# The first block of a time-mix and FFN kernel: parameters as rows, roots on ScalarE, mixing in eight steps

## The chip, the cores and the metric

The kernel runs on one core of a Trainium2 chip. It drives five engines that run side by side and wait for each other through semaphores: TensorE (PE in the profile; PEld is its weight load), VectorE (DVE), ScalarE (ACT), GpSimd (POOL) and SyncE (SP), which here issues every transfer from memory. The metric is the device time of one execution in microseconds (us). Smaller is better.

## The reference

Input x has 4 sequences of 1024 tokens with 512 channels. Cut to what matters:

```
xn  = layernorm(x)                               # no gamma, no beta
xx  = shift(xn) - xn                             # the token before; the first token takes the second
k   = (xn + xx * time_mix_k) @ Wk.T              # 512 -> 704
r   = (xn + xx * time_mix_r) @ Wr.T
state_t = state_(t-1) * exp(-exp(time_decay)) + relu(k_t)    # along time
att = layernorm((state * r) @ Wv.T) * ln_gamma + ln_beta
ffn = gelu(fp16(xn) @ W0.T + bias0).fp16 @ W1.T + bias1      # 512 -> 2048 -> 512
out = x + att + fp16(ffn)
```

## The kernel before

Tokens go through in eight blocks of 512, two per sequence. For each block channels lie on the partitions, so the normalized x must be turned. In blocks 1 to 7 VectorE does this in 32x32 pieces during the FFN of the block before. Block 0 has nothing to hide behind, and has a path of its own: TensorE turns 128x128 pieces into four PSUM banks `pts`, and the mixing reads these banks.

The loads at the start, all on one queue (cut):

```python
    x_now = load_x(0)                       # four transfers of 128 x 512
    ...
    nc.vector.memset(w_sb, 0.0)
    nc.sync.dma_start(mk_sb, mix_k.rearrange("(c p) -> p c", p=P))   # channel on the partition
    nc.sync.dma_start(mr_sb, mix_r.rearrange("(c p) -> p c", p=P))
    for c in range(NC):                     # NC = 4
        nc.sync.dma_start(wk_sb[c], wkT[c * P : (c + 1) * P, :])
        nc.sync.dma_start(wr_sb[c], wrT[c * P : (c + 1) * P, :])
    nc.sync.dma_start(w_sb[:, :NF], decay[:H0].rearrange("(c p) -> p c", p=P))
    nc.sync.dma_start(w_sb[:HF, NF:], decay[H0:].rearrange("(c p) -> p c", p=HF))
    nc.sync.dma_start(b0_sb, bias0.rearrange("(c p) -> p c", p=P))
```

The first block's statistics, normalization and mixing (cut):

```python
    def rstd_of(var, name):                 # 1/sqrt as a power, on GpSimd
        nc.gpsimd.tensor_scalar_add(r, var, EPS)
        nc.gpsimd.tensor_tensor(r, r, nhalf[:, :n], ALU.pow)

    # first_inputs: statistics of four tiles s on VectorE, rstd_of once for each two tiles
        for s in range(NS):                 # NS = 4
            normalize(xs[:, s, :], ...)     # VectorE, (x - mean) * rstd
            for c in range(NC):
                nc.tensor.transpose(pts[c][:, s * P : (s + 1) * P], xs[:, s, c * P : (c + 1) * P], ident)
        for rest, m in ((onemk_sb, mk_sb), (onemr_sb, mr_sb)):
            nc.vector.tensor_scalar(rest, m, -1.0, 1.0, ALU.mult, ALU.add)     # 1 - m
        for c, pt in enumerate(pts):
            parts = (xk with mk_sb, onemk_sb), (xnT with mr_sb, onemr_sb)      # shortened
            for dst, part, m, rest in parts:
                nc.scalar.activation(part, pt, AF.Identity, scale=rest)
            for dst, part, m, rest in parts:                                   # first token
                nc.scalar.activation(dst[:, 0:1], pt[:, 1:2], AF.Identity, bias=part[:, 0:1], scale=m)
            for dst, part, m, rest in parts:
                nc.vector.scalar_tensor_tensor(dst[:, 1:], pt[:, : TB - 1], m, part[:, 1:], ALU.mult, ALU.add)
```

Then ScalarE copies the banks to fp16 (`x16`) and their last column to `last`, takes the two exponentials of the decay, and the products of the attention begin. For each h of 5 there are four products for k, four for r; relu on ScalarE, the scan and the product with r on VectorE:

```python
        for h in range(NF):
            for c in range(NC):
                product(pk, wk_sb, cols, xk[:, c, :], c)
            st = states(h, P, pk)           # relu on ScalarE, scan on VectorE
            for c in range(NC):
                product(pr, wr_sb, cols, xnT[:, c, 1:], c)
            nc.vector.tensor_mul(g[:, h, :], st, pr)
        # then the last half h, both parts in one bank: pkr
```

PSUM has eight banks, used as two pools of four: `ps_mm` for products, `ps_e` for the turned x and later the FFN's output. Behind the weights of the attention, W0 and W1 come in as raw tiles of 128x512 (three buffers, `w0raw` and `w1raw`), and ScalarE and VectorE split each in two parts while the first attention runs:

```python
    def split(hi, lo, raw):
        nc.scalar.copy(hi, raw)
        nc.vector.tensor_sub(lo, raw, hi.bitcast(F32))
```

Of the kernel before, what the change touches and what calls it, by code (L numbers as in the profile page):

```python
# [9 lines left out]
F32 = mybir.dt.float32  # L10
F32R = mybir.dt.float32r
AF = mybir.ActivationFunctionType
ALU = mybir.AluOpType

P = 128
EPS = 1e-5
# [3 lines left out]
def time_mix_and_gelu_ffn(  # L20
# [26 lines left out]
    nc = tc.nc  # L47
# [3 lines left out]
    TB = 512  # L51
    NS = TB // P
    NC = C // P
    NN = N // P
# [3 lines left out]
    NF = HID // P  # L58
    H0 = NF * P
    HF = P // 2  # L60
# [3 lines left out]
    def pool(name, bufs, **kw):  # L64
        return ctx.enter_context(tc.tile_pool(name=name, bufs=bufs, **kw))
# [4 lines left out]
    const = pool("const", 1)  # L70
    one = pool("one", 1)
    two = pool("two", 2)
    three = pool("three", 3)
    four = pool("four", 4)
    ps_mm = pool("ps_mm", 4, space=bass.MemoryType.PSUM)
# [12 lines left out]
    ident = const.tile([P, P], F32, name="ident")  # L88
# [1 line left out]
    nhalf = const.tile([P, NS], F32, name="nhalf")  # L90
    nc.vector.memset(nhalf, -0.5)

    mk_sb = const.tile([P, NC], F32, name="mk_sb")
    mr_sb = const.tile([P, NC], F32, name="mr_sb")
    w_sb = const.tile([P, NF + 1], F32, name="w_sb")
    nc.vector.memset(w_sb, 0.0)
    b0_sb = const.tile([P, NN], F32, name="b0_sb")

    nc.sync.dma_start(mk_sb, mix_k.rearrange("(c p) -> p c", p=P))
    nc.sync.dma_start(mr_sb, mix_r.rearrange("(c p) -> p c", p=P))  # L100
    wk_sb = [const.tile([P, HID], F32, name=f"wk_{c}") for c in range(NC)]
    wr_sb = [const.tile([P, HID], F32, name=f"wr_{c}") for c in range(NC)]
    for c in range(NC):
        nc.sync.dma_start(wk_sb[c], wkT[c * P : (c + 1) * P, :])
        nc.sync.dma_start(wr_sb[c], wrT[c * P : (c + 1) * P, :])
    nc.sync.dma_start(w_sb[:, :NF], decay[:H0].rearrange("(c p) -> p c", p=P))
    nc.sync.dma_start(w_sb[:HF, NF:], decay[H0:].rearrange("(c p) -> p c", p=HF))
    nc.sync.dma_start(b0_sb, bias0.rearrange("(c p) -> p c", p=P))

    onemk_sb = const.tile([P, NC], F32, name="onemk_sb")  # L110
    onemr_sb = const.tile([P, NC], F32, name="onemr_sb")

    wv_sb = const.tile([P, NF + 1, C], F32, name="wv_sb")
    gamma_sb = const.tile([P, C], F32, name="gamma_sb")
    beta_sb = const.tile([P, C], F32, name="beta_sb")
# [48 lines left out]
    xnT = const.tile([P, NC, TB + 1], F32, name="xnT")  # L164
# [3 lines left out]
    def rstd_of(var, name):  # L168

        n = var.shape[1]  # L170
        r = two.tile([P, n], F32, tag=f"rstd{n}", name=name)
        nc.gpsimd.tensor_scalar_add(r, var, EPS)  # L172
        nc.gpsimd.tensor_tensor(r, r, nhalf[:, :n], ALU.pow)
        return r

    def stats_of(mv, s, src, name):
        st6 = two.tile([P, 6], F32, tag="st6", name=name)
        nc.vector.bn_stats(st6, src)  # L178
        nc.vector.bn_aggr(mv[:, s, :], st6)  # L179

    def normalize(dst, src, mean, rstd):
        nc.vector.tensor_scalar(dst, src, mean, rstd, ALU.subtract, ALU.mult)
# [21 lines left out]
    def first_inputs(xs, behind):  # L204

        pts = [ps_e.tile([P, TB], F32, tag="pe", name=f"pt_0_{c}") for c in range(NC)]
        mv = two.tile([P, NS, 2], F32, tag="mv", name="mvx_0")
        rstds = []  # L210
        with tc.manual_schedule(engines={nc.gpsimd.engine}):
            for s0 in range(0, NS, 2):
                for s in (s0, s0 + 1):
                    stats_of(mv, s, xs[:, s, :], f"stx_0_{s}")
                rstds.append(rstd_of(mv[:, s0 : s0 + 2, 1], f"rx_0_{s0}"))
        xk = one.tile([P, NC, TB], F32, tag="xk", name="xk_0")
        with tc.manual_schedule(engines={nc.scalar.engine, nc.vector.engine}):
            for s in range(NS):
                normalize(
                    xs[:, s, :],  # L220
                    xs[:, s, :],
                    mv[:, s, 0:1],
                    rstds[s // 2][:, s % 2 : s % 2 + 1],
                )
                for c in range(NC):
                    nc.tensor.transpose(
                        pts[c][:, s * P : (s + 1) * P], xs[:, s, c * P : (c + 1) * P], ident
                    )
            for rest, m in ((onemk_sb, mk_sb), (onemr_sb, mr_sb)):
                nc.vector.tensor_scalar(rest, m, -1.0, 1.0, ALU.mult, ALU.add)  # L230
            for c, pt in enumerate(pts):
                ar = two.tile([P, TB], F32, tag="xx", name=f"ar_0_{c}")
                parts = (
                    (xk[:, c, :], xk[:, c, :], mk_sb[:, c : c + 1], onemk_sb[:, c : c + 1]),
                    (xnT[:, c, 1:], ar, mr_sb[:, c : c + 1], onemr_sb[:, c : c + 1]),
                )
                for dst, part, m, rest in parts:
                    nc.scalar.activation(part, pt, AF.Identity, scale=rest)
                for dst, part, m, rest in parts:

                    scaled = nc.scalar.activation(
                        dst[:, 0:1], pt[:, 1:2], AF.Identity, bias=part[:, 0:1], scale=m
                    )
                for dst, part, m, rest in parts:
                    mixed = nc.vector.scalar_tensor_tensor(  # L245
                        dst[:, 1:], pt[:, : TB - 1], m, part[:, 1:], ALU.mult, ALU.add
                    )

        behind.enter_context(tc.issue_after(scaled.ins))
        behind.enter_context(tc.issue_after(mixed.ins))  # L250
        x16s = []
        for c, pt in enumerate(pts):
            x16 = four.tile([P, TB], F16, tag="x16", name=f"x16_0_{c}")
            nc.scalar.copy(x16, pt)
            x16s.append(x16)
            nc.scalar.copy(last[:, c, :], pt[:, TB - 1 :])
        return x16s, xk

    def mixed_inputs(i):
# [23 lines left out]
    def ffn_input(i, x16s):  # L283
        xf = wide.tile([P, NC, TB], F32R, tag="xf", name=f"xf_{i}")
        for c in range(NC):
            nc.vector.tensor_copy(xf[:, c, :], x16s[c])
        return xf
# [164 lines left out]

    behind = ExitStack()
    x16s, xk = first_inputs(x_now, behind)

    nc.scalar.activation(w_sb, w_sb, AF.Exp)
    nc.scalar.activation(w_sb, w_sb, AF.Exp, scale=-1.0)
    xf = ffn_input(0, x16s)
    for i in range(len(blocks)):
        more = i + 1 < len(blocks)  # L460
# [25 lines left out]
        if more:  # L486
            x16s, xk = state["mixed"]
# [46 lines left out]
```

## Time and profile before

| | |
|---|---|
| time, median of three runs | 949.51 us (948.9 to 949.73) |
| span of the profiled execution | 947.2 us |
| mean granted clock of TensorE | 0.997 |
| TensorE busy, matmul | 931.0 us, 98% |
| VectorE busy | 485.7 us, 51% |
| ScalarE busy | 160.5 us, 17% |
| GpSimd busy | 53.7 us, 6% |
| moved by DMA | 106.47 MB, mean 112 GB/s |

How to read what the prediction shows. In the page, a row of digits is the span in 40 equal slices, each digit the busy share in tenths. The chain of waits is followed back from the last instruction; each of its lines is a start, a duration and what ran or was waited for. A line of the timeline is a start, a duration, the engine, the source line, the operation, output<-inputs, shapes and a count; in brackets stands the idle time before it and what ended that. A product in fp32 appears as two matmul rows. Names such as `xk` stand for the program's tiles, and `L238` for a line of the program.

### The profile page before, as it was taken

Reading aid. Unit: us, or ns where it says so; the run is one execution under the profiler, and the core shown is the slowest. Engines: PE = TensorE matmul, PEld = TensorE weight load, DVE = VectorE, ACT = ScalarE, POOL = GpSimd, SP = SyncE. Lnnn points to the kernel's source line nnn. Section 1 sums busy time; section 2 is a strip of 40 time slices with the busy share of each in tenths; the row PEclk is TensorE's granted clock in tenths of the full one; section 3 lists DMA queues with packets and bytes.
Section 4 is the critical chain, followed back from the end, with each engine's and each line's share of the span. In section 5 each row is a group of like instructions: output and inputs, shape, how many; then the busy total and the mean of one; then the engine's idle time right before and its main releaser. Section 6 shows DMA issues by size and latency. Waiting matters only on the chain.

```text
span 947.2 us, 8658 instructions
## 1 busy us (share of the span) xinstructions
PE 931.0 (98%) x3216; PEld 583.0 (62%) x3216; DVE 485.7 (51%) x836; ACT 160.5 (17%) x264; POOL 53.7 (6%) x128
## 2 busy tenths in 40 slices
PE   5999999999999999999999999999999999999998
PEld 2447764478644785448854488545884458744686
DVE  6558852385424844259443593436924269232513
ACT  5322321012100121002201022010210102111021
POOL 1011000010001000011000100001000020000100
PEclk9999999999999999999999999999999999999999
DMA  8734570045400354004540155301542024410243
GB/s 271 240 133 145 209 268 1 0 134 199 157 0 21 136 186 148 0 24 142 190 134 1 33 165 180 111 1 57 184 161 88 0 80 143 160 62 0 69 153 111
DMA packets 43368, 106.47 MB, mean 112 GB/s; under 512 B 8256, under 2 KB 8256, under 8 KB 43328
## 3 DMA queue, kind: packets, MB, share of 16 engines
q1 hardware_dynamic: 43328, 105.94, 33.4%
q8 instruction: 25, 0.41, 0.2%
q14 instruction: 15, 0.12, 0.0%
HBM read 89.14 MB, written 16.78 MB: 112 GB/s over the span
## 4 chain that ended last, share of the span: by engine, by line
PE 93%; DVE 4%; ACT 1%; issue 1%; DMA 0%; POOL 0%; DVEq 0%
PE pd L408 23%; PE pe L423 22%; PE po L348 15%; PE pr L313 15%; PE pk L313 14%; PE pkr L313 3%; PE po L358 2%; DVE xnT L199 1%; DVE w L120 1%; DVE stx L178 0%; DVE d L418 0%; DMA x<-in_L_attn_x 0%; DVE z L395 0%; DVE e L394 0%; DVE xk L278 0%
## 5 line engine op out<-in xcount | busy, mean ns | idle before, releaser
L423 PE MATMUL pe<-w,d 128*128 128x512 f32 x1024 | 251.2, 390 | 1.4 <-DVE w L120 0.8
L423 PEld LDWEIGHTS pe<-w,d 128*128 128x128 f32 x1024 | 192.2, 188 | 42.4 <-DVE d L418 1.5
L408 PE MATMUL pd<-xf,w0h 128*128 128x512 f32 x512 | 203.8, 398 | 0.0
L408 PE MATMUL pd<-xf,w0l 128*128 128x512 f32 x512 | 199.9, 390 | 0.0
L416 ACT ACTIVATE d<-pd,b_sb 128x512 f16<-128x512 f32 x128 | 87.9, 686 | 418.2 <-PE pd L408 399.2
L313 PE MATMUL pk<-xk,wk 128*128 128x512 f32 x320 | 145.9, 599 | 3.1 <-DVE xk L245 3.1
L313 PE MATMUL pr<-xnT,wr 128*128 128x512 f32 x320 | 144.0, 592 | 0.0
L348 PE MATMUL po<-wv_sb,g 128*128 128x512 f32 x320 | 140.8, 595 | 0.0
L418 DVE CAST d<-d 128x512 fp32r<-128x512 f16 x128 | 54.1, 424 | 130.7 <-ACT d L416 129.7
L408 PEld LDWEIGHTS pd<-xf,w0h 128*128 128x128 f32 x512 | 96.2, 188 | 28.0 <-issue 5.7
L408 PEld LDWEIGHTS pd<-xf,w0l 128*128 128x128 f32 x512 | 96.2, 188 | 21.6 <-issue 1.9
L313 PEld LDWEIGHTS pk<-xk,wk 128*128 128x128 f32 x320 | 61.0, 192 | 78.3 <-issue 70.9
L313 PEld LDWEIGHTS pr<-xnT,wr 128*128 128x128 f32 x320 | 60.7, 190 | 76.8 <-issue 76.1
L348 PEld LDWEIGHTS po<-wv_sb,g 128*128 128x128 f32 x320 | 60.2, 190 | 75.5 <-issue 74.8
L199 DVE STREAM_TRANSPOSE xnT<-x 32x512 f32<-32x512 f32 x112 | 78.7, 703 | 2.2
L300 DVE TENSOR_TENSOR_SCAN st<-w_sb,carry,rk 128x512 f32<-128x512 f32 (+1 forms) x24 | 30.8, 1282 | 70.2 <-ACT rk L298 70.2
L298 ACT ACTIVATE rk<-pk 128x512 f32<-128x512 f32 x40 | 24.0, 600 | 232.9 <-PE pk L313 232.9
L178 DVE BATCH_NORM_STATS2 sty<-po 128x6 f32<-128x512 f32 x32 | 22.1, 690 | 73.4 <-PE po L358 67.9
L300 DVE TENSOR_TENSOR_SCAN st<-w_sb,rk 128x512 f32<-128x512 f32 (+1 forms) x24 | 29.3, 1222 | 53.6 <-ACT rk L298 53.5
L324 DVE TENSOR_TENSOR g<-st,pr 128x512 f32<-128x512 f32 x40 | 27.5, 688 | 53.7 <-PE pr L313 53.6
L172 POOL TENSOR_SCALAR ry<-mvy 128x1 f32<-128x1 f32 x32 | 11.4, 357 | 503.4 <-DVE mvy L179 503.4
L313 PE MATMUL pkr<-xnT,wr 128*64 128x512 f32 x64 | 29.2, 598 | 0.0
(56 smaller groups left out, 439.6 us busy)
## 6 DMA issues: line engine op xcount, KB each, us to landing
w<-w1d SPq DMA_DIRECT2D x111, 512.0 KB, 3.2
x<-in_L_attn_x SPq DMA_DIRECT2D x32, 256.0 KB, 3.4
xres<-in_L_attn_x SPq DMA_DIRECT2D x32, 256.0 KB, 2.7
w1d<-w SPq DMA_DIRECT2D x16, 512.0 KB, 3.0
out<-z SPq DMA_DIRECT2D x32, 256.0 KB, 4.8
w0raw<-in_L_ffn_W SPq DMA_DIRECT2D x16, 256.0 KB, 4.5
w1raw<-in_L_ffn_W SPq DMA_DIRECT2D x16, 256.0 KB, 3.5
wk<-in_L_attn_Wk SPq DMA_DIRECT2D x4, 352.0 KB, 6.0
```

Of the source, the lines that this page charges most:

```text
L178: nc.vector.bn_stats(st6, src)
L199: nc.vector.transpose(dst[i * Q : (i + 1) * Q, :, :, j, :], src[j * Q : (j + 1) * Q, :, :, i, :],)
L298: nc.scalar.activation(rk[:hw], pk, AF.Relu)
L300: nc.vector.tensor_tensor_scan(st[:hw], w_sb[:hw, h : h + 1].to_broadcast([hw, TB]), rk[:hw], 0.0 if t0 == 0 else carry[:hw, h : h + 1], A ...
L313: nc.tensor.matmul(dst, w[c][:, cols], src, start=(c == 0), stop=(c == NC - 1))
L324: nc.vector.tensor_mul(g[:, h, :], st, pr)
L348: nc.tensor.matmul(pos[s], g[:, h, s * P : (s + 1) * P], wv_sb[:, h, :], start=(first and h == 0), stop=(not first and h == NF - 1),)
L358: nc.tensor.matmul(pos[s], gh[rows, s // 2, :], wv_sb[rows, NF, :], start=first, stop=not first)
L408: nc.tensor.matmul(pd, w[c][:, cols], xf[:, c, :], start=(c == 0 and w is w0h), stop=(c == NC - 1 and w is w0l),)
L416: nc.scalar.activation(d16, pd, AF.Gelu, bias=b0_sb[:, n : n + 1])
L418: nc.vector.tensor_copy(d, d16)
L423: nc.tensor.matmul(pe[s], d[:, s * P : (s + 1) * P], w1[part], start=(n == 0 and part == 0), stop=(n == NN - 1 and part == 1),)
```

## The change

It touches only the path of block 0, and what is loaded ahead of it. Its purpose is to bring the first product of the attention forward, and to keep TensorE's clock up until then.

- The mix vectors, the decay and bias0 are loaded as rows (4 to 16 rows of 128 values) right behind x, ahead of the weights, turned on TensorE and copied by ScalarE, where before they were loaded with the channel on the partition.
- The block's inverse deviations come from a square root on ScalarE and a reciprocal on VectorE. The table for the root is loaded by a first root that nothing reads. Tile 0 is normalized on ScalarE, the others on VectorE.
- The first token, which takes its neighbour from the other side, is treated by five small VectorE instructions on two columns that TensorE turned apart (`edge`), where before ScalarE had two one-column instructions for each c.
- The mixing goes in eight steps, one ScalarE and one VectorE instruction each, ordered so that the two engines read different banks: (c, kind) in the order of `steps`, kind 0 for k and 1 for r. The scheduler orders the first eight products to match: k of c = 0, 1, r of 0, 1, k of 2, 3, r of 2, 3.
- Nineteen products of the identity with itself go to a bank that nothing reads: 13 at the start, 1 behind tile 0, 5 behind tile 3.
- The four banks of `ps_mm` are taken by the unread products and the three turned parameters and edges first, then by the products of the attention. The exponentials of the decay move behind the copies of the banks.

The diff, cut:

```diff
+    eps_sb = const.tile([P, 1], F32, name="eps_sb")
+    mix_rows = const.tile([2 * NC, P], F32, name="mix_rows")
+    late_rows = const.tile([NF + 1 + NN, P], F32, name="late_rows")
-    nc.sync.dma_start(mk_sb, mix_k.rearrange("(c p) -> p c", p=P))
-    nc.sync.dma_start(mr_sb, mix_r.rearrange("(c p) -> p c", p=P))
+    nc.sync.dma_start(mix_rows[:NC], rows(mix_k))
+    nc.sync.dma_start(mix_rows[NC:], rows(mix_r))
+    nc.sync.dma_start(late_rows[:NF], rows(decay[:H0]))
+    nc.sync.dma_start(late_rows[NF : NF + 1, :HF], decay[H0:].rearrange("(c p) -> c p", p=HF))
+    nc.sync.dma_start(late_rows[NF + 1 :], rows(bias0))
     ...                                    # wk, wr as before
-    (decay and bias0 behind the weights)
 ...
+        def busy(n):
+            for _ in range(n):
+                nc.tensor.matmul(idle[:, :P], ident, ident, start=True, stop=True)
+        def deviations(s0):
+            nc.scalar.activation(rstd[:, s0 : s0 + 2], mv[:, s0 : s0 + 2, 1], AF.Sqrt, bias=eps_sb)
+        def inverses(s0):
+            nc.vector.reciprocal(rstd[:, s0 : s0 + 2], rstd[:, s0 : s0 + 2])
+        def normalized(s):                  # s == 0: shift0 on VectorE, then Identity on ScalarE
+        steps = [(0, 0), (1, 0), (0, 1), (1, 1), (2, 0), (3, 0), (2, 1), (3, 1)]
+            nc.scalar.activation(shift0, eps_sb, AF.Sqrt)
+            busy(13)
+            stats(0); stats(1); deviations(0); stats(2); inverses(0)      # one per line in the source
+            normalized(0); turned(0)
+            (edge: four transposes of two tokens)
+            busy(1)
+            stats(3); deviations(2); normalized(1)
+            nc.scalar.copy(ends, edge_t)
+            turned(1)
+            nc.tensor.transpose(mix_t, mix_rows, ident[: 2 * NC, : 2 * NC])
+            nc.scalar.copy(mix_sb, mix_t)
+            nc.scalar.activation(rest_sb, mix_t, AF.Identity, bias=1.0, scale=-1.0)
+            inverses(2); normalized(2); turned(2); normalized(3); turned(3)
+            nc.tensor.transpose(late_t, late_rows, ident[: NF + 1 + NN, : NF + 1 + NN])
+            busy(5)
+            (five small VectorE instructions for the first token)
+            for c, kind in steps:
+                nc.scalar.activation(part, pts[c][:, 1:], AF.Identity, scale=rest_sb[:, j : j + 1])
+                nc.vector.scalar_tensor_tensor(dst, pts[c][:, : TB - 1], mix_sb[:, j : j + 1], part, ALU.mult, ALU.add)
 ...                                        # x16 and last as before, then
+        nc.scalar.activation(w_sb, late_t[:, : NF + 1], AF.Exp)
+        nc.scalar.activation(w_sb, w_sb, AF.Exp, scale=-1.0)
+        nc.scalar.copy(b0_sb, late_t[:, NF + 1 :])
```

More of the change, by code (lines that the diff above doesn't have):

```diff
@@ L91, in time_mix_and_gelu_ffn, with rows @@
     nc.vector.memset(nhalf, -0.5)
-    mk_sb = const.tile([P, NC], F32, name="mk_sb")
-    mr_sb = const.tile([P, NC], F32, name="mr_sb")
+    eps_sb = const.tile([P, 1], F32, name="eps_sb")
+    nc.vector.memset(eps_sb, EPS)
+    mix_rows = const.tile([2 * NC, P], F32, name="mix_rows")
+    late_rows = const.tile([NF + 1 + NN, P], F32, name="late_rows")
+    nc.vector.memset(late_rows, 0.0)
+    mix_sb = const.tile([P, 2 * NC], F32, name="mix_sb")
+    rest_sb = const.tile([P, 2 * NC], F32, name="rest_sb")
     w_sb = const.tile([P, NF + 1], F32, name="w_sb")
-    nc.vector.memset(w_sb, 0.0)
     b0_sb = const.tile([P, NN], F32, name="b0_sb")
-    nc.sync.dma_start(mk_sb, mix_k.rearrange("(c p) -> p c", p=P))
-    nc.sync.dma_start(mr_sb, mix_r.rearrange("(c p) -> p c", p=P))
+    mk_sb, mr_sb = mix_sb[:, :NC], mix_sb[:, NC:]
+    def rows(ap):
+        return ap.rearrange("(c p) -> c p", p=P)
+    nc.sync.dma_start(mix_rows[:NC], rows(mix_k))
[3 more added lines that the diff above has]
+    nc.sync.dma_start(late_rows[NF + 1 :], rows(bias0))
     wk_sb = [const.tile([P, HID], F32, name=f"wk_{c}") for c in range(NC)]
@@ L105, in time_mix_and_gelu_ffn @@
         nc.sync.dma_start(wr_sb[c], wrT[c * P : (c + 1) * P, :])
[L106 to L111, printed above, removed]
     wv_sb = const.tile([P, NF + 1, C], F32, name="wv_sb")
@@ L208, in first_inputs @@
         pts = [ps_e.tile([P, TB], F32, tag="pe", name=f"pt_0_{c}") for c in range(NC)]
-        mv = two.tile([P, NS, 2], F32, tag="mv", name="mvx_0")
[L210 to L215, printed above, removed]
-        xk = one.tile([P, NC, TB], F32, tag="xk", name="xk_0")
@@ L217, in first_inputs @@
[L217 to L223, printed above, removed]
-                )
[L225 to L235, printed above, removed]
-                )
[L237 to L247, printed above, removed]
@@ new lines, in first_inputs @@
+        idle = ps_mm.tile([P, TB], F32, tag="mm", name="idle")
+        small = ps_mm.tile([P, TB], F32, tag="mm", name="small")
+        tail = ps_mm.tile([P, TB], F32, tag="mm", name="tail")
+        mix_t = small[:, : 2 * NC]
+        late_t = tail[:, : NF + 1 + NN]
+        edge = ps_mm.tile([P, TB], F32, tag="mm", name="edge")
+        edge_t = edge[:, : NC * 2].rearrange("p (c t) -> p c t", t=2)
+        mv = two.tile([P, NS, 2], F32, tag="mv", name="mvx_0")
+        rstd = two.tile([P, NS], F32, tag=f"rstd{NS}", name="rx_0")
@@ new lines, in first_inputs, with stats @@
+        shift0 = const.tile([P, 1], F32, name="shift0")
+        ends = const.tile([P, NC, 2], F32, name="ends")
+        xk = one.tile([P, NC, TB], F32, tag="xk", name="xk_0")
+        def busy(n):
+            for _ in range(n):
+                nc.tensor.matmul(idle[:, :P], ident, ident, start=True, stop=True)
+        def stats(s):
+            stats_of(mv, s, xs[:, s, :], f"stx_0_{s}")
+        def deviations(s0):
+            nc.scalar.activation(
+                rstd[:, s0 : s0 + 2], mv[:, s0 : s0 + 2, 1], AF.Sqrt, bias=eps_sb
+            )
@@ new lines, in inverses, with turned @@
+        def inverses(s0):
+            nc.vector.reciprocal(rstd[:, s0 : s0 + 2], rstd[:, s0 : s0 + 2])
+        def normalized(s):
+            x_s, r = xs[:, s, :], rstd[:, s : s + 1]
+            if s == 0:
+                nc.vector.scalar_tensor_tensor(shift0, mv[:, 0, 0:1], -1.0, r, ALU.mult, ALU.mult)
+                nc.scalar.activation(x_s, x_s, AF.Identity, bias=shift0, scale=r)
+            else:
+                normalize(x_s, x_s, mv[:, s, 0:1], r)
+        def turned(s):
+            for c in range(NC):
+                nc.tensor.transpose(
+                    pts[c][:, s * P : (s + 1) * P], xs[:, s, c * P : (c + 1) * P], ident
+                )
@@ new lines, in first_inputs @@
+        steps = [(0, 0), (1, 0), (0, 1), (1, 1), (2, 0), (3, 0), (2, 1), (3, 1)]
+        with tc.manual_schedule(
+            engines={nc.scalar.engine, nc.vector.engine, nc.tensor.engine}
+        ):
+            nc.scalar.activation(shift0, eps_sb, AF.Sqrt)
+            busy(13)
+            stats(0)
+            stats(1)
+            deviations(0)
+            stats(2)
+            inverses(0)
+            normalized(0)
+            turned(0)
+            for c in range(NC):
+                nc.tensor.transpose(
+                    edge_t[:, c, :], xs[:2, 0, c * P : (c + 1) * P], ident[:2, :2]
+                )
+            busy(1)
+            stats(3)
+            deviations(2)
+            normalized(1)
+            nc.scalar.copy(ends, edge_t)
[3 more added lines that the diff above has]
+            nc.scalar.activation(rest_sb, mix_t, AF.Identity, bias=1.0, scale=-1.0)
+            inverses(2)
+            normalized(2)
+            turned(2)
+            normalized(3)
+            turned(3)
+            nc.tensor.transpose(
+                late_t, late_rows, ident[: NF + 1 + NN, : NF + 1 + NN]
+            )
+            busy(5)
+            apart = two.tile([P, NC], F32, tag="apart", name="apart")
+            nc.vector.tensor_sub(apart, ends[:, :, 1], ends[:, :, 0])
+            for dst, m in ((xk[:, :, 0], mk_sb), (xnT[:, :, 1], mr_sb)):
+                part = two.tile([P, NC], F32, tag="part", name="part")
+                nc.vector.tensor_mul(part, apart, m)
+                nc.vector.tensor_add(dst, part, ends[:, :, 0])
+            for c, kind in steps:
+                if kind == 0:
+                    dst = part = xk[:, c, 1:]
+                else:
+                    ar = two.tile([P, TB], F32, tag="xx", name=f"ar_0_{c}")
+                    dst, part = xnT[:, c, 2:], ar[:, 1:]
+                j = kind * NC + c
+                scaled = nc.scalar.activation(
+                    part, pts[c][:, 1:], AF.Identity, scale=rest_sb[:, j : j + 1]
+                )
+                mixed = nc.vector.scalar_tensor_tensor(
+                    dst, pts[c][:, : TB - 1], mix_sb[:, j : j + 1], part, ALU.mult, ALU.add
+                )
@@ L454, in time_mix_and_gelu_ffn @@
     x16s, xk = first_inputs(x_now, behind)
-    nc.scalar.activation(w_sb, w_sb, AF.Exp)
-    nc.scalar.activation(w_sb, w_sb, AF.Exp, scale=-1.0)
     xf = ffn_input(0, x16s)
```

## The prediction

> **What bounds the kernel now.** I read the page first, then the chain of waits over the first 24 us, then the busy table by single microseconds there, then the instruction order of both versions, last the timeline of VectorE and ScalarE up to 58 us.
>
> ```profile
> PE 931.0 (98%) x3216; PEld 583.0 (62%) x3216; DVE 485.7 (51%) x836; ACT 160.5 (17%) x264; POOL 53.7 (6%) x128
> PE   5999999999999999999999999999999999999998
> ...
> PE 93%; DVE 4%; ACT 1%; issue 1%; DMA 0%; POOL 0%; DVEq 0%
> ```
>
> TensorE is full everywhere but in the first slice. The chain repeats from block to block: its pr groups stand at 136.64 and 252.21 us, 115.57 apart, while the first block's stands at 19.46, so that block takes 117.18 to the same point. What the change can reach is the head before 22.89, where h=1 begins.
>
> ```profile
> 0.72 2.82 DMA x<-in_L_attn_x
> 3.55 0.02 issue
> 3.57 0.71 DVE stx L178
> ...
> 7.47 0.87 POOL rx L173
> 8.34 0.03 issue
> 8.36 1.00 DVE x L182 x2
> 9.37 0.08 DVE onemk_sb L230
> 9.45 0.08 DVE onemr_sb L230
> 9.53 0.00 issue
> 9.53 0.85 ACT L238
> 10.37 0.45 issue
> 10.82 0.69 ACT xk L238
> ...
> 17.53 0.76 DVE xk L245
> 18.29 0.04 issue
> 18.33 1.13 PE pk L313 x2
> 19.46 3.44 PE pr L313 x8
> 22.89 1.29 PE pk L313 x3
> ```
>
> The reader is to see four things in a row: GpSimd's power of -0.5 ends at 8.34 and holds up normalization; a ScalarE table load starts only at 9.53 and ends at 10.82; mixing runs in ScalarE's pace from 10.82 to 18.3; and all four pr products come after it.
>
> ```profile
> 13.00:14.00 1.00, 0.59 (x1) 0.42 (x2) 1.00 (x2) 1.00 (x4) 0.00 (x0) 0.76 1.12 287
> 14.00:15.00 1.00, 1.00 (x2) 0.00 (x0) 0.77 (x3) 1.00 (x3) 0.00 (x0) 0.50 1.15 14
> 15.00:16.00 1.00, 1.00 (x2) 0.50 (x2) 0.77 (x2) 1.00 (x4) 0.00 (x0) 0.50 0.61 117
> 16.00:17.00 1.00, 1.00 (x3) 0.31 (x2) 1.00 (x2) 1.00 (x3) 0.00 (x0) 0.53 0.72 205
> 17.00:18.00 1.00, 0.95 (x3) 0.13 (x1) 0.77 (x2) 1.00 (x6) 0.00 (x0) 1.00 0.94 297
> ```
>
> After the time come the busy sums of PE, PEld, DVE, ACT and POOL, then clock, DMA share and GB/s. Two things: the clock is half from about 13.75 to 17.15, after the 2.7 us that PE stood idle before 13.41; and between 14 and 15 the DMA engines are fully busy while moving 14 GB/s, which is the decay and bias0 load in pieces of 4 bytes.
>
> **What the Trainium skill says.** "TensorE: Matmul & The Clock Gate", Part 1, has the clock at half speed until a free-running window of about 3.4 us has been busy, and half again after an idle one. The trace agrees: one fp32 product (two matmul rows) takes 2 x 0.86 us at 14 us and 0.86 us later (3.44 for four). The same page's Part 4 says that PE transposes do not bring the clock up; the trace differs: after 15 transposes spaced 0.21 us and nothing else, the last takes 0.27 us instead of 0.42. "ScalarE: Activation LUTs", What ACT_TABLE_LOAD costs, gives about 1.28 us for a load, and its section on table sets puts sqrt and exp into different sets; the load here takes 1.283 us. "DMA: Bandwidth & Descriptors", Specifications, wants 512 B or more per piece; the 14 GB/s agree.
>
> **The change part by part.** Time of each step in the changed kernel:
>
> Start. x lands as before, statistics start at 3.57 and the second aggregate ends at 5.27 (0.80 us a tile). The square-root table load (1.28) begins near 0.7 and is hidden. Square root on ScalarE: 0.36, from the 0.367 of the small exponential, so 5.7. VectorE finishes its third tile at 6.07; reciprocal and shift, two instructions of about 0.16 (the onemk row), end at 6.35. ScalarE scales tile 0: 0.69 plus 0.09 for one more pointer operand, an estimate, so 6.4 to 7.2. VectorE meanwhile does the fourth tile's statistics (to 7.1), tile 1 (0.5, to 7.55), the second reciprocal (7.75), tiles 2 and 3 (0.48 each, to 8.8). Before, tile 3 was done at 9.36: 0.55 us gained, although the first tile comes no earlier than before.
>
> First mixing step. Four transposes per tile, 0.11 at full clock; the first of tile 3 is out at about 9.2 (8.85 + 0.27 + a hop). The small mix parameters are 8 rows of 512 B, on the chip by about 6, turned on PE behind tile 1 and copied by ScalarE before 8.9. No table load stands here any more: ScalarE starts at 9.25 instead of 10.82, ends 9.95; VectorE 10.0 to 10.75 (0.75); PE starts at 10.8. Before, this was 13.41, as VectorE waited also for both one-column instructions of ScalarE. Gain here 2.6 us: 1.57 from the start of ScalarE, about 1.05 from the first step.
>
> Pace of mixing. Before, a chunk c costs ScalarE 0.58 + 0.58 + 0.24 + 0.24 = 1.64 us and gives one k and one r input; 4 x 1.64 = 6.6. Now the one-column instructions are gone (five tiny VectorE instructions on edges stand instead, before 9.6 and so hidden), ScalarE needs 0.58 and VectorE 0.66 per step (12.61 to 13.27), and they use different banks at the same time. Eight steps: VectorE from 10.0 to 15.35.
>
> TensorE. The order now is k0 k1 r0 r1 k2 k3 r2 r3, each product released by its own step. At full clock a product is 0.86, longer than the 0.66 of a step, so PE sets the pace: 10.8 + 8 x 0.86 = 17.7 for the start of h=1, against 22.89. **Gain 5.2 us** for everything after.
>
> Unread products. 13 at the start: 128 columns at 0.86/4 = 0.21 each warm, 0.43 cold, 5.6 us if all cold, from the identity at 1.3 to 6.9, just where tile 0 arrives. One and five more fill gaps around 8 and 9.4 to 10.5. All lie in time in which PE waits; their worth is the clock, which before was half for 3.4 us.
>
> Weights. The wk, wr issues move back by three small ones, 1.5 us (5.1 for the first, 3.60 before), but before, the queue also moved only 76 GB/s from 5 to 6 for the 4-byte mix loads. First landing about 8.6 (8.4 before), then one each 0.9 us as before (wk landed at 8.4, 10.2, 12.0, 13.8), the last about 15. Products need them at 10.8, 11.7 ... 16.8: covered.
>
> Exponential. Its table load moves behind the x16 copies: 1.28 us more on ScalarE, but that is at 16.4 instead of 17.3 + 2.3, so the first relu is at about 18.3 and the first scan near 19.3 (20.39 before). PE does not wait for it before the third h.
>
> **Rivals.** (1) The splitting of W0 does not follow.
>
> ```profile
> 26.71 1.97 ACT L119 CAST w0h<-w0raw 128x512 fp32r<-128x512 f32 x3 [4.81 <-DMA w0raw<-in_L_ffn_W]
> ...
> 51.86 0.62 ACT L119 CAST w<-w1raw 128x512 fp32r<-128x512 f32 x1 [1.54 <-DMA w1raw<-in_L_ffn_W]
> 52.39 0.59 ACT L298 ACTIVATE rk<-pk 128x512 f32<-128x512 f32 x1
> ```
>
> Three raw buffers go round through DMA, ScalarE and VectorE, and relus, scans and g stand in the same in-order queues. rk_4 runs at 52.39 although its product is done at 46.9; g_4 ends at 55.13, and attention output uses it at 57.7: 2.6 us of slack. Shifting PE by 5.2 eats that unless the stream too comes forward by 2.6. For it: 1.5 us of 4-byte traffic vanish, wv, gamma, beta and x are queued earlier, the first split begins 1 us earlier, the second round's landings 2.4. Following the rounds by hand gives 1.5 to 3 us of lead near the end, and the new order puts st_4 before the third w1 split. So 0 to 2 us given back, 0.5 expected: 949.5 - 4.7. If the stream kept its times exactly: 947.
>
> (2) The clock falls to half in the products all the same, as the window runs free and PE is only some 60 to 80% busy between 7 and 10.8. A half window in 10.8 to 17.7 costs 3.4/2 = 1.7. I give it 1 in 5: 0.3 expected; alone it makes 946.
>
> (3) Mixing stays with the engines: VectorE and ScalarE disturb each other in PSUM and a step takes 0.9. Then the last is at 17.2 and h=1 at 18.1, only 0.4 worse.
>
> (4) Weights come late, 1.5 us behind: the last product waits to 16.9, nothing lost.
>
> Later blocks keep their order. The 1.06 us that PE waits at 111 and 113 follow from a VectorE chain that starts at the end of attention output (77.2), so it moves along.
>
> **Range and chances.** 949.5 - 5.2 + 0.5 + 0.3 = 945.1; I say 945.0. Both rivals at full size give 947.2; none and a start 0.7 earlier give 943.6. 2% is 19 us, more than the whole head can give, so "within 2%" is nearly sure.
>
> **What would show it.** Right: the first pk at about 10.8, h=1 near 17.7, clock 1.0 from 8 us on, all further pk and pr groups without gaps and about 5 us earlier. Wrong: a half clock after 10.8; waits of po or pd on VectorE or ScalarE between 45 and 60 us; a first scaling step of ScalarE later than 9.6, by the mix rows or the edge copies; the span shrinking by less than h=1's start moved.

## The result, and the profile after

| | before | changed |
|---|---|---|
| time, median (lowest to highest) of six runs each, side by side | 949.66 us (948.90 to 950.26) | 944.71 us (944.26 to 946.58) |
| span of the profiled execution | 947.2 us | 943.0 us |
| start of h=1 in block 0 | 22.89 us | 19.12 us |
| first k group of block 1 | 133.21 us | 129.42 us |

The ratio is 0.995, with a 95% interval of 0.9937 to 0.9963: a real gain of half a per cent, well inside 2%.

The page of the changed kernel, its busy sums and its row of slices for TensorE:

```profile
PE 934.3 (99%) x3260; PEld 587.2 (62%) x3260; DVE 485.9 (52%) x842; ACT 162.7 (17%) x265; POOL 51.7 (5%) x124
...
PE   8999999999999999999999999999999999999998
```

TensorE's sum is 3.3 us larger although the kernel is shorter: unread products count as busy. Only the first digit differs, 8 for 5. So the page says where to look, the head, and nothing of how much was won there.

The chain of waits of the changed kernel over the first 24 us (start, duration, what ran or was waited for):

```profile
3.93 2.87 DMA late_rows<-in_L_ffn_bias
6.79 0.82 ACT x L248
...
7.66 0.66 PE pt L254 x4
8.32 0.34 PE edge L275 x4
8.65 0.42 PE idle L231 x2
9.07 0.44 PE pt L254 x4
9.51 0.15 PE small L284
9.66 1.02 PE pt L254 x8
...
10.85 1.31 PE idle L231 x10
12.16 1.80 PE pk L385 x4
...
19.12 3.43 PE pk L385 x8
```

The chain has gone over to TensorE, which from 7.66 on never stands still. Most of this is work that something waits for: the transposes of tiles 0 to 3 with edges, one unread product and the rows of parameters between them (7.66 to 10.85), and the eight mixed products in 6.96 us (to 19.12). The five unread products between the two only hide a wait, as the timeline shows (start, duration, instruction; in brackets the idle time before it and who ended that):

```profile
10.46 1.26 ACT L310 ACTIVATE xk<-pt,rest_sb 128x511 f32<-128x511 f32 x2 [0.51 <-PE pt L254]
12.00 1.96 PE L385 MATMUL pk<-xk,wk 128*128 128x512 f32 x4
```

ScalarE's first mixing step starts at 10.46, as soon as the first piece of tile 3 is turned, and VectorE's ends at 11.92. The first product starts at 12.00; the chain has it at 12.16, as it counts from the modelled end of the unread product before. So the head is the queue of transposes, then one mixing step of both engines, then eight products. Of the head's gain nothing was given back later: h=1 moved by 22.89 - 19.12 = 3.77 us, block 1 by 133.21 - 129.42 = 3.79. The spans differ by 0.4 us more, which comes at about 0.05 us a block over the later blocks (115.52 for 115.57). They run the same instructions, and the cause is open.

One microsecond of the busy table, columns as in the prediction:

```profile
14.00:15.00 1.00, 1.00 (x3) 0.38 (x2) 1.00 (x3) 0.68 (x2) 0.00 (x0) 1.00 1.02 387
```

In this microsecond the kernel before moved 14 GB/s at half clock; now it is 387 at full clock.

### The profile page after: what moved, and what is told of

It reads as the page before. It is cut to its first block, busy times and chain, and to the rows that moved or that the text cites. A ratio compares the mean times of both kernels' runs of the same rounds, so it can differ in the third digit from the quotient of the medians.

```text
span 943.0 us, 8746 instructions
## 1 busy us (share of the span) xinstructions
PE 934.3 (99%) x3260; PEld 587.2 (62%) x3260; DVE 485.9 (52%) x842; ACT 162.7 (17%) x265; POOL 51.7 (5%) x124
## 4 chain that ended last, share of the span: by engine, by line
PE 94%; DVE 4%; issue 1%; DMA 0%; SPq 0%; ACT 0%; POOL 0%; DVEq 0%
PE pd L480 23%; PE pe L495 22%; PE po L420 15%; PE pr L385 15%; PE pk L385 15%; PE pkr L385 3%; PE po L430 2%; DVE xnT L204 1%; DVE w L125 0%; DVE d L490 0%; DMA late_rows<-in_L_ffn_bias 0%; DVE z L467 0%; DVE e L466 0%; DVE xk L350 0%; DVE xnT L350 0%
## 5 line engine op out<-in xcount | busy, mean ns | idle before, releaser
L466 DVE TENSOR_TENSOR e<-pe,b_sb 128x512 f16<-128x512 f32 x32 | 20.8, 685 | 17.0 <-PE pe L495 17.0
```

The lines of the kernel that those rows point to most:

```text
L466: nc.vector.tensor_add(e16, pe, b1_sb)
```

## The experiments

All change one thing in the changed kernel, unless said otherwise. Each was timed beside the kernel before on its own chip; that had medians of 949.67, 949.63 and 949.81 in the three sets, and a ratio is always to it. "Block 1" is the start of its first k group, the place where everything the head won or lost has been settled. Both starts are those of the chain of waits; the timeline has h=1 some 0.17 us earlier. In same_bank the products of h=1 have no common start.

| | time, us | ratio, 95% interval | h=1 | block 1 |
|---|---|---|---|---|
| again | 944.92 (944.76 to 945.07) | 0.9948 (0.9935 to 0.9962) | 19.18 | 129.44 |
| no_unread | 948.44 (945.94 to 949.51) | 0.9986 (0.9979 to 0.9992) | 23.16 | 133.42 |
| no_thirteen | 948.19 (947.35 to 949.78) | 0.9985 (0.9978 to 0.9992) | 22.51 | 132.83 |
| no_five | 945.37 (944.38 to 947.26) | 0.9949 (0.9935 to 0.9962) | 20.70 | 131.79 |
| no_one | 944.72 (944.18 to 944.79) | 0.9947 (0.9935 to 0.996) | 18.98 | 129.24 |
| columns | 946.60 (944.49 to 947.35) | 0.9963 (0.995 to 0.9975) | 18.82 | 131.44 |
| same_bank | 945.56 (945.09 to 945.72) | 0.9956 (0.9944 to 0.9969) | - | 130.01 |
| power | 944.72 (944.63 to 945.10) | 0.9949 (0.9937 to 0.9962) | 19.06 | 129.63 |
| early_recip | 944.13 (944.07 to 944.74) | 0.9942 (0.9929 to 0.9954) | 18.22 | 128.81 |
| early_recip_b | 944.32 (944.09 to 945.42) | 0.9943 (0.993 to 0.9955) | 18.52 | 128.81 |
| best4 | 944.10 (943.89 to 944.20) | 0.9942 (0.9928 to 0.9955) | 18.13 | 128.41 |
| best4_b | 944.16 (944.10 to 944.45) | 0.994 (0.9927 to 0.9952) | 18.36 | 128.67 |

**The changed kernel again.** No edit.

> The changed kernel once more, as the measure for its variants. Theory: of the gain, the start of h=1 explains all but some 0.4 us, so the second k group starts at 19.1 +- 0.3 us again and the time is 944.7 +- 0.4. The clock stays at full speed in most executions; one in five or six has a half window and is 1.5 to 2.5 us longer. Rival (part of the gain comes from later blocks): blocks 1 to 7 repeat in clearly less than 115.5 us.

Its h=1 and block 1 stand within 0.06 us of the first trace. So 3.8 us of the gain lie in the head in both. None of these five executions is a longer one, where one in five or six was expected.

**Without the unread products.**

```diff
-            busy(13)
-            busy(1)
-            busy(5)
-        idle = ps_mm.tile([P, TB], F32, tag="mm", name="idle")
```

> All 19 unread products left out, all else as changed. Theory (they are worth their clock): TensorE starts cold at the first transpose, 16 transposes, edges and rows take 0.21 instead of 0.11 us each, and part of the first eight products run at half clock; h=1 starts at 20.4 to 22 instead of 19.1, the time is 1.3 to 3 us longer, 946 to 948. Rival (they only stand in TensorE's queue): the queue is 0.6 us shorter, h=1 at 18.5, the time 0.6 us shorter.

About 3.5 us are lost of a gain of 4.9, more than I had given the products. The chain of waits of this kernel, its first products:

```profile
13.22 3.78 PE pk L376 x4
17.00 2.72 PE pr L376 x4
19.73 1.72 PE pk L376 x4
```

Four matmul rows, two products, take 1.72 us at full clock. The first four rows take 3.78, the next 2.72; only the third group has full speed. Before that, the transposes are slow as well: each lasts 0.42 us or more, where those of the changed kernel have 0.27, and the first product starts 1.2 us later than in the changed kernel (13.22 for 12.00 in the timeline). With h=1 at 23.16 this head is even later than that of the kernel before. The 21 runs spread over 3.6 us; the changed kernel's five spread over 0.3 and its first six over 2.3, so the spread says little.

**Which of the unread products it is.** One kernel without `busy(13)`, one without `busy(5)`, one without `busy(1)`.

> Only the thirteen unread products at the start are left out. Theory (they carry the clock): TensorE stands idle until tile 0 arrives at 6.7 to 7.0 us, so the transposes run at half speed (0.28 instead of 0.11 to 0.14 us), the first product starts near 13.0 and at least its first 3 to 4 us run at half clock; h=1 starts at 21.5 to 23 instead of 19.1, and the time is 947 to 948.5, with a spread of over 2 us between executions. Rival (the products at 8.6 and at 10.8 to 12.2 do it as well, since they bridge the gap between transposes and products): clock full from the first product on, h=1 at 19.5 to 20, time 945.0 to 945.8.

The thirteen at the start carry nearly all of it: 3.3 to 3.5 us. The size came out as the theory had it, the mechanism did not. The chain of waits:

```profile
7.63 1.09 PE pt L254 x4
...
11.01 1.90 PE pt L254 x8
...
13.13 2.43 PE idle L231 x10
15.56 1.79 PE pk L384 x4
```

The first product runs at full speed here, and starts 3.4 us late. Tile 0 was scaled even 0.12 us earlier than in the changed kernel, so no engine held TensorE up. Its own queue did, at half speed: tile 0 takes 1.09 for 0.66, edges and the one unread product 1.24 for 0.76, tile 1 0.85 for 0.44, tiles 2 and 3 1.90 for 1.02, the five unread ones 2.43 for 1.31. These alone make 3.3 us. The five at the end hold up the product here: VectorE's first step ends at 13.83, and the product starts at 15.36 in the timeline. And the busy table of this kernel shows nothing of the half speed:

```profile
12.00:13.00 1.00, 1.00 (x6) 0.67 (x4) 0.00 (x0) 0.64 (x2) 0.00 (x0) 1.00 1.00 375
```

The granted clock stands at 1.00 in a microsecond in which every transpose takes twice its time. The reason is in the trace: its first record of the clock comes at 15.59 us, just when the spacing of rows goes over to full speed, and the column counts the time before any record as full. So it shows a clock taken back, not one that has not come up yet; the spacing of equal instructions shows both. In no_unread the first record comes at 18.90 us, and all 21 executions have a mean clock of 0.999 or more.

The Trainium skill says in "TensorE: Matmul & The Clock Gate", Part 4, that transposes do not bring the clock up. In the prediction I held the trace of before against it. The experiments put both in proportion: without the unread products, transposes, edges and rows left the array slow for 4.7 us, and without the thirteen for 5.4 and the five behind them too. In the kernel before, sixteen bare transposes in a row did end in three fast ones (0.27 us), from 10.15 on. What decides between the two is open: the edges, two columns each, stood in the slow queues and not in that one, and the array comes up at another time in each execution (4.40 to 7.49 us in the eleven traces that have the thirteen).

> Only the five unread products behind tile 3 are left out. Theory (the thirteen carry the clock, the five only bridge 1.3 us): the first product no longer waits for them and starts at 11.95 instead of 12.16; h=1 at 18.9 to 19.0, time 0.1 to 0.2 us under the changed kernel's 944.8, with now and then an execution 1.5 to 2 us longer. Rival (the 1.3 us gap without them lets the clock fall in most executions): first products at half clock, h=1 at 20.5 to 21, time 946 to 947.

The median lies between the two expectations; the rival's 946 to 947 did not come, nor a gain. The profile fell on the longest of the five executions and shows the danger that I had put elsewhere. The busy table, 10 to 11 us:

```profile
10.00:11.00 1.00, 1.00 (x6) 0.64 (x5) 0.08 (x1) 0.24 (x2) 0.00 (x0) 0.50 1.01 313
```

The clock was half from about 9.0 to 12.4: in the transposes, ahead of where the five would have stood, and after a gap (6.50 to 7.96) no longer than that of the changed kernel (5.99 to 7.66). A further 0.5 us is lost near 56 us, where TensorE waits for g. So this trace says nothing against leaving them out. It does show that leaving them out can gain nothing in the head:

```profile
12.04 1.26 ACT L309 ACTIVATE xk<-pt,rest_sb 128x511 f32<-128x511 f32 x2 [1.07 <-PE pt L254]
13.57 1.98 PE L384 MATMUL pk<-xk,wk 128*128 128x512 f32 x4 [0.85 <-DVE xk L312]
```

From ScalarE's first step to the first product it is 1.53 us without the five, with TensorE waiting, and 1.54 with them (10.46 to 12.00). The theory, that the product waited for them, was wrong. What they do for the clock stays open.

> Only the one unread product behind tile 0 left out. Theory (TensorE's queue is what tile 3 waits for): the transposes of tile 3 end 0.4 us earlier (10.3 instead of 10.7), h=1 at 18.8, of which 0.1 to 0.4 us are seen in the time; the clock stays up. Rival 1 (normalization decides): h=1 at 19.1, time the same. Rival 2 (it kept the clock up): a half window in several executions, 1.5 to 2.5 us longer each.

0.2 us by block 1, and 0 to 0.2 by time, less than its interval can prove. The clock stayed up.

**The reciprocal ahead of the third tile's statistics.**

```diff
-            stats(2)
             inverses(0)
             normalized(0)
+            stats(2)
```

> Reciprocal, shift and scaling of tile 0 moved ahead of the statistics of tile 2 on VectorE. Theory (the reciprocal stood behind statistics that waited for x): shift ready near 5.7 us, ScalarE scales tile 0 from 5.8 instead of 6.8, TensorE turns it from 6.7, is no longer behind when tile 3 comes (9.2), ScalarE's first mixing step at 9.9 instead of 10.46, h=1 at 18.5, the time 0.6 us shorter, 944.1. Rival (the scaling waits for the landing of the bias0 rows, which the chain of waits names): scaling stays at 6.8 us, h=1 at 19.1, the time the same.

The timeline of VectorE in the changed kernel shows why:

```profile
5.60 0.69 DVE L183 BATCH_NORM_STATS2 stx<-x 128x6 f32<-128x512 f32 x1 [0.55 <-DMA x<-in_L_attn_x]
6.33 0.18 DVE L184 BATCH_NORM_AGGREGATE mvx<-stx 128x2 f32<-128x6 f32 x1
6.43 0.13 DVE L242 RECIPROCAL rx<-rx 128x2 f32<-128x2 f32 x1
```

The root was ready at 5.38, but the reciprocal stands in VectorE's queue behind statistics that wait for the third part of x. With the order changed, the timeline of ScalarE has tile 0's scaling 0.91 us earlier:

```profile
5.88 0.81 ACT L248 ACTIVATE x<-x,shift,rx 128x512 f32<-128x512 f32 x1 [0.43 <-DMA late_rows<-in_L_ffn_bias]
```

The releaser named there, and in the chain of the changed kernel above, is the landing of bias0, which this instruction does not read. It moved with VectorE's shift (ends at 5.84 here, 6.76 there), so VectorE was what it waited for; in the next experiment, where bias0 is loaded much later, the scaling starts at 6.80 and the shift is named. h=1 came 0.90 us earlier, block 1 0.61.

**The parameters as columns again.** The loads as in the kernel before, decay and bias0 behind the weights; no rows turned on TensorE.

```diff
-    nc.sync.dma_start(mix_rows[:NC], rows(mix_k))
+    nc.sync.dma_start(mk_sb, mix_k.rearrange("(c p) -> p c", p=P))
...                                # mr likewise; wk, wr; then
+    nc.sync.dma_start(b0_sb, bias0.rearrange("(c p) -> p c", p=P))
-            nc.tensor.transpose(mix_t, mix_rows, ident[: 2 * NC, : 2 * NC])
```

> Small parameters loaded as before (channel on the partition, decay and bias0 behind the weights), so no turning of rows; all else as changed. Theory (rows serve the transfers, not the head): h=1 at 18.8 to 19.2, but decay and bias0 hold the DMA engines for some 2 us behind the weights, the splits of W0 come 1 to 2 us later, g of h=4 ends at 53.4 to 54.4 instead of 52.4, just when attention output needs it (54.0): time 0 to 0.5 us longer than the changed kernel. Rival A (the rows carry much of the gain): 1.5 us or more longer, with TensorE waits near 50 to 60 us. Rival B (the rows delay x and turn on the critical queue for nothing): 0.3 us or more shorter.

The head itself gains 0.3 us, as TensorE has fewer small things in its queue. But 35 us later the timeline of TensorE has two waits that the changed kernel does not have:

```profile
53.26 0.50 PE L465 MATMUL pd<-xf,w0h 128*128 128x512 f32 x1 [1.30 <-ACT rk L355]
...
55.80 8.85 PE L405 MATMUL po<-wv_sb,g 128*128 128x512 f32 x20 [0.43 <-DVE g L381]
```

Block 1 starts 2.0 us later, and the median is 1.7 us longer, though one of the five runs took only 944.49. The loads hold up W0 behind them: ScalarE splits its fourth raw tile at 30.19 instead of 27.22. Relu and g stand in the queues behind the splits. "DMA: Bandwidth & Descriptors" in the Trainium skill, Rules for kernel authors, says of strided last dimensions that such a load becomes one descriptor per element. That agrees. The pages of this kernel and of the changed one count their packets:

```profile
DMA packets 43369, 106.49 MB, mean 113 GB/s; under 512 B 8256, under 2 KB 8256, under 8 KB 43328
DMA packets 39573, 106.49 MB, mean 113 GB/s; under 512 B 4431, under 2 KB 4460, under 8 KB 39532
```

Under 512 B there are 3825 more, and the parameters are 3776 values. From 13.5 to 14.5 us the DMA engines are fully busy and move 42 GB/s. From 15 to 16 they move 3 and are 9% busy; what they wait for there is not shown. The edit puts decay and bias0 into columns and behind the weights at once; the two were not tried apart. The rows pay here, 35 us later, and not in the head.

**The steps one bank after the other.**

```diff
-        steps = [(0, 0), (1, 0), (0, 1), (1, 1), (2, 0), (3, 0), (2, 1), (3, 1)]
+        steps = [(c, kind) for c in range(NC) for kind in range(2)]
```

> The eight steps in the order k, r of c = 0, then of c = 1 and so on, so that two steps in a row read the same bank; the scheduler puts products of h=1 between those of h=0. Theory (readers of one bank go one after the other, ScalarE waits for VectorE): two steps take about 2.05 us instead of 1.41, the last mixing step ends near 19.4 instead of 16.9, but TensorE fills with products of h=1, so the k group of h=2 starts 0.2 to 0.5 us later than 26.0 and the time is 0.2 to 0.5 us longer. Rival A (the banks don't matter): pitch 1.4, same time. Rival B (TensorE can't fill): 2 us or more longer.

ScalarE's timeline in this kernel, the second step of the first bank:

```profile
11.93 0.69 ACT L310 ACTIVATE ar<-pt,rest_sb 128x511 f32<-128x511 f32 x1 [0.82 <-DVE xk L313]
```

It waits until VectorE has read the same bank. Two steps take 2.16 us instead of 1.41, more than the 1.72 of their two products, so the two engines in turn set the pace. TensorE loses less than that, as the scheduler lets products of h=1 in between: 0.6 us at block 1, 0.6 to 0.9 in time.

**The power on GpSimd again.** In place of the roots and reciprocals; ScalarE loads the table of exp at the start, and the second table load is gone.

> The inverse deviations of block 0 again as a power on GpSimd (0.23 to 0.45 plus 0.72 to 0.87 us for two tiles), the first ScalarE table being the one for exp, so that no second load stands behind the copies; all else as changed. Theory (the roots as such bring nearly nothing, as TensorE's queue decides when tile 3 is turned): tile 0 scaled near 6.6 us, tiles 2 and 3 normalized at 8.5 to 9.5, tile 3 turned as late as now, h=1 at 18.8 to 19.3, the first scan 1 us earlier, time within 0.4 us of 944.9. Rival (the roots carry the earlier normalization): h=1 at 19.7 or later and the time 0.6 us or more longer.

The time is that of the changed kernel. The power takes 0.72 us for two tiles (and the sum before it 0.23), and tile 0's scaling came at 6.74 for 6.79, since VectorE's queue held the reciprocal back anyway. The table load that ended at 10.82 in the kernel before was in the way there only because the first mixing step was ScalarE's first instruction; where a first one that nothing reads brings the table early, the power would have done. Block 1 is 0.2 us later: the scheduler then set st_4 behind a split, g_4 ends at 53.97, and attention output, which starts at 54.03, takes 8.85 us for 8.59.

**A version that takes what the others showed.** Early reciprocal, no single unread product, four at the end, and a fourth raw buffer.

```diff
+            inverses(0)
+            normalized(0)
             stats(2)
-            inverses(0)
-            normalized(0)
...
-            busy(1)
-            busy(5)
+            busy(4)
-   (three tiles) tag="raw", name=...)
+   (three tiles) tag="raw", name=..., bufs=4)
```

> Reciprocal ahead of tile 2's statistics, no unread product behind tile 0, four instead of five behind tile 3, and four raw buffers instead of three for the splits of W0 and W1. Theory (the head has 1.2 us left, and what was given back near 53 us is the raw buffers' round): h=1 at 17.8 to 18.0, no wait of TensorE between 45 and 60 us, time 943.3 to 943.7. Rival (the round is bound by landing, not by buffers): the same head, but attention output starts at 53.1 to 53.4 as with the early reciprocal alone and the time is 944.0 to 944.3.

The head is better by 1.0 us than that of the changed kernel, and at the attention output, where early reciprocal had needed 8.85 us, it needed 8.59. The chain of early reciprocal shows the wait (g_4 ended at 53.13 in its timeline), and that of best4 has none:

```profile
53.15 0.04 issue
53.19 8.85 PE po L420 x20
...
53.07 8.59 PE po L419 x20
```

In time it is level with early reciprocal, so both were measured again, side by side.

> The kernel with the early reciprocal again, beside the next one on the same chip. From the first time: h=1 at 18.2, attention output takes 0.26 us longer than 8.59 us as the stream of W0 and W1 has lost its lead; 944.1.

> Early reciprocal, the one unread product at tile 0 left out, four instead of five at the end, four raw buffers instead of three: again. Theory (the fourth raw buffer takes back what early reciprocal lost at the attention output, 0.3 us): 943.7 to 943.9, 0.2 to 0.4 us under early reciprocal. Rival (no gain in time, as in the first comparison): the same as early reciprocal within 0.1 us, 944.1.

944.32 and 944.16 with overlapping runs: the fourth buffer is worth nothing that the time shows. Nor was the 8.85 us there the second time: early reciprocal had h=1 0.30 us later, 8.59 us of attention output, and block 1 at 128.81 again. The equal block 1 from two heads is a coincidence. From h=1 to block 1 it is 110.3 us in the changed kernel, in the second trace of early reciprocal and in both of best4, and 110.6 only in the first of early reciprocal, where the attention output had to wait for g_4. So only that trace shows a bound behind the head, and best4's block 1 (128.41 and 128.67) is earlier because its head is. In the set that held both, early reciprocal's slowest run (944.74) is below the changed kernel's fastest (944.76), 0.8 us lie between the medians; the intervals of their ratios, which hold the spread of the kernel before, overlap.

## Why the prediction was right, point by point

The path was right in the main: the table load is out of the way, the products and no longer ScalarE set the pace of the mixing, and the unread products keep the clock up. The power on GpSimd, which the prediction names first, is no bound with the rest changed: with it back the time is the same. That the total (945.0 for 944.71) came so close is luck. The head gained 1.4 us less than put down; 0.8 us allowed for rivals were not lost; and the medians lie 1.2 us further apart than the head moved, which the prediction did not have. The steps:

- **First tile (7.2).** Ended at 7.60. Root, reciprocal, shift and scaling took what I had put down for them, within 0.1 us (0.30, 0.13, 0.16 and 0.81). The wait for x before the third tile's statistics (0.55 us) was not in the sum; early_recip shows that it was not needed at all.
- **First mixing step (9.25).** This is the term that failed: 10.46. I let the last transposes follow their tile, and did not add up TensorE's queue. It runs without a gap from 7.66 to 10.69 with 3.03 us of work, while tile 3 was normalized at 9.14. Of the 1.21 us some 0.3 go back to this tile (8.8 was put down), the other 0.9 to the queue. early_recip shows it: tile 3 comes only 0.10 us earlier there, but the transposes start 0.91 earlier, and the first step comes as much earlier (9.55).
- **First product (10.8).** 12.00 in the timeline. The step from ScalarE's start to the product took what I had said (1.54 us for 1.55).
- **Pace (8 x 0.86).** Right: 6.96 us. The engines' steps, 0.70 each where 0.58 and 0.66 were put down, stay below, and same_bank shows that this hangs on the order of banks.
- **Gain in the head (5.2).** 3.77. Of the 1.42 us that are missing, 1.20 are the first product's and 0.07 the pace's. The rest is no time: the sum took the first product from the timeline and the 22.89 from the chain, which has the same start 0.16 later.
- **Rival 1, the splitting (0.5 given back).** Nothing was given back. g_4 ends at 52.36 and attention output begins at 54.04: 1.7 us of the 2.6 us of slack are left. The mechanism is there: columns turns it on at 2.0 us. With the changed loads it doesn't bind in this trace; in those of power and of the first early reciprocal the slack is used up.
- **Rival 2, a half clock (1 in 5, 1.7 us).** One of the six executions took 946.58, 1.9 above the median, at a mean clock of 0.998; the others had 0.999 or more. The size and the share fit, and the no_five execution with its one half-speed window has the same mean clock; that this one had such a window is not shown, as its trace was not taken. Where a trace shows such a window (no_five), it lies in the transposes, ahead of the products. In the kernel before, it lies at 13.52 to 16.94, not at 13.75 to 17.15: the rows of 0.76 and 0.53 say so. Nothing hangs on this.
- **Rival 3, the engines' pace.** Did not happen as 0.9 a step, but same_bank makes 1.08 out of 0.70.
- **Rival 4, weights.** No product waits for one.
- **Exponential (first scan near 19.3).** 20.49. The copies of x16 (2.3) and the table load (1.28, 18.33 to 19.61) took what I had put down; the copies ended at 18.33 instead of 16.4, as the mixing began 1.2 us later and ScalarE's steps go at VectorE's pace. It cost nothing, as I had said.
- **Unread products.** "Their worth is the clock" was right and has now a size: 3.5 us, without which the change would bring 1.2. What such products would bring in the kernel before, alone, was not tried.

That leaves 3.8 us in the trace for 4.9 in the medians. 0.4 is the even drift over the blocks. The rest is that the profiled execution of before (949.0) is one of its fastest, 0.7 below its median; why its executions spread by 1.4 us was not tried.

The parts do not add up to the gain: undoing one takes away 3.5 (unread products), 1.7 to 2.0 (rows), 0.6 to 0.9 (order of banks) or 0 (roots): some 6 us, of a gain of 4.9. So they depend on each other. Probably rows clear the stream that an earlier head would run into, and a full clock makes TensorE the bound in the first place; two parts were never undone together. What the edges and tile 0 on ScalarE are worth was not tried.

## What to carry to other kernels

Where a chain ends in TensorE's own queue, add up the queue, small instructions too, at the speed that the clock will have there; some products without use while the engine would stand idle can be worth more than everything that is moved (3.5 us of 4.9 here). Do not take the last thing in the chain for a cost: ask whether the next would have started sooner without it. Before sizing a step, read what stands ahead of it in its engine's order and what that waits for: a reciprocal of 0.13 us behind statistics of data not yet there cost 0.9. When a head comes forward, look for the next thing that depends on a stream and not on the head, and make the stream come forward too.

## What the runs showed of the hardware

- The first record of the clock in a trace comes when the rows of TensorE go over to half their spacing (0.21 to 0.11 us for 128 columns): at 4.47 us in the changed kernel, 10.11 in the one before, 15.59 in no_thirteen, 18.90 in no_unread. Ahead of it the granted clock reads 1.00 although the array is slow; 0.50 stands only where the array was up and fell (before from 13.52, no_five from 8.97, 3.41 us each).
- Thirteen products of 128 columns from 1.34 us on brought the array up between 4.40 us (no_one) and 7.49 (power, where all thirteen ran slow) in eleven traces. In the changed kernel it stayed up through a gap of 1.67 us; in no_five it fell after one of 1.46. Transposes with edges and rows between them, then five products, left it slow for 8.0 us in no_thirteen (7.63 to 15.59).
- Readers of one PSUM bank on ScalarE and VectorE went one after the other (0.82 and 0.90 us of waiting). Whether this is the bank itself or the program's dependencies was not tried.
- A load of 4-byte pieces takes about one packet for each value: 3825 more packets under 512 B in columns than in the changed kernel, for 3776 values.
